# The part of the scan output that depends only on silu(z), computed among the scan inputs and added to x there

## Chip, core and metric

The kernel runs on one core of a Trainium2 chip. The metric is device time in microseconds of one execution; lower is better. Before the change it was 9031.49 us, the median of 3 runs (9028.09 to 9043.99).

## What is computed

Four layers run one after the other on 4 images of 64 x 64 tokens with 128 channels, all in f32: a Mamba-like block (layer 0), self-attention (layer 1), a convolution block (layer 2) and neighbourhood attention with an MLP (layer 3). The change lies in layer 0. Cut to what matters:

```python
xz = _ln(input) @ in_proj_w
x_, z = jnp.split(xz, 2, axis=-1)
xc = silu(depthwise_conv3x3(x_) + conv_b)
# four directions k: delta, B, C from xc; h = exp(delta*A)*h + delta*xc*B ; y_k = sum_n h*C
y = sum of the four directions, each put back in image order, plus Ds * xc
y = _ln(y, onorm_w, onorm_b)          # (y - mean) * rstd * onorm_w + onorm_b
y = y * silu(z)
x = input + y @ out_proj_w
x = x + gelu(_ln(x) @ fc1_w + fc1_b) @ fc2_w + fc2_b
```

The kernel splits `y @ out_proj_w` into two sums. With c the centred y, it is `rstd * ((c * onorm_w * silu(z)) @ out_proj_w) + (onorm_b * silu(z)) @ out_proj_w`. The second sum, called `pb` in the kernel, does not depend on the scan.

## The kernel before

**Program and order.** `network` (L1620) writes the whole program for one core, without loops on the chip. A scheduling layer then decides, from its own estimate of times and from priorities, in which order each engine's instructions stand; on the chip each engine works its queue in that order and waits on semaphores. A tile pool gives out buffers in turn; a tile that needs a buffer waits until all uses of the one before have ended.

**Stages.** `scan_inputs` (L277) makes, for one image, everything the scan needs, in 8 chunks of 512 tokens: layer norm (`layernorm_T`, L178), in_proj, the 3x3 convolution on TensorE with diagonal weights (L247), Silu (L359 for z into `sz`, L376 for `xc`), the projections to delta, B and C (`steps`, L296), and it stores `sz`, `xc`, `delta`, `du` and `bc` to DRAM. `selective_scan` (L438) runs the four directions in the order 0, 1, 3, 2, in units: one unit is a product dB on POOL (L485), two exponentials on ACT (L491), two scans on DVE (L493), and the product with C, on DVE (L498) or POOL (L506). TensorE sums over the state with the `pick` matmuls of L539. The last direction runs backwards, so the y of chunk 7 is the first to be finished. `scan_output` (L565) takes y, `sz` and x of each chunk from DRAM, chunk 7 first, two chunks interleaved, and makes the norm, the gate, out_proj, the second layer norm and the MLP (`mlp`, L212); meanwhile it also steps through `layer3_mlp` (L1552) of the image before. `rest` (L1588) is `scan_output`, `layer1`, `layer2` and layer 3's attention (`layer3_attention`, L1216) of one image.

**How they lie together.** The scans of the four images follow one another and have the high priority base `SCAN_FIRST` written around them. `scan_inputs` of image 0 comes first; those of images 1 to 3 are issued next to the scan of image 0, and `rest` of image i next to the scan of image i + 1. `rest` of image 3 and its MLP of layer 3 come after the last scan.

**Queues and buffers.** SP issues the loads of both stages and of the scan (`dt` and `du` L468, `bc` L476, `y_before` L520 to L530), the stores of `du` (L332), and the loads of x (L338 in `scan_inputs`, L594 in `scan_output`). ACT issues the stores of `sz`, `xc`, `bc` and `delta`. `bc`, `dt`, `du` and `dB` have 4 buffers each; the pool of `scan_inputs`, in which x lies, has 2. The scan holds 4 PSUM banks (3 `dA`, 1 `py`), the other stage 4, shared by all its tiles with the tag `ps`.

**The Silus.** `Together` (L100) gathers the activations of a chunk that need another table (Silu of z of chunk c, Silu of the convolution of chunk c - 1) and lets them run only after the last of their matmuls.

**The lines that the change touches.** In `scan_inputs` the weights are loaded at L288 to L291, x at L338, and `sz` is stored at L382. In `scan_output` the weights are loaded at L576 and L577, L580 scales `out_proj` by `onorm_b` on DVE, L594 loads x. L612 sums the squares (`pv`), L621 makes `pb`, L625 the gated part `pg`, L628 adds `pb` to x on DVE, and L630 adds `rstd * pg`.

Of the kernel before, what the change touches and what calls it, by code (L numbers as in the profile page):

```python
# [28 lines left out]
F32 = mybir.dt.float32  # L29
# [13 lines left out]
LC = 512  # L43
# [213 lines left out]
def token_tiles(dram, c):  # L257

    return dram[span(c), :].rearrange("(t p) c -> p t c", p=128)
# [17 lines left out]
def scan_inputs(tc, K, A, D, img):  # L277

    nc = tc.nc
    with ExitStack() as ctx:
        pool = ctx.enter_context(tc.tile_pool(name="si_a", bufs=2))
        wpool = ctx.enter_context(tc.tile_pool(name="si_aw", bufs=1))
        psum = ctx.enter_context(tc.tile_pool(name="si_ap", bufs=4, space=PSUM))
        load = loader(tc, wpool, A, 0)
        ln_w, ln_b = load("ln1_w", [128, 1]), load("ln1_b", [128, 1])  # L288
        in_proj, conv_b = load("in_proj_w", [128, 2 * DI]), load("conv_b", [128, ND])
        diag = load("conv_diag", [128, ND, 9, 128], D.conv_diag)  # L290
        x_proj, dt_w = load("x_proj_w", [128, ND, 2, 128]), load("dt_w", [128, 2, DI])  # L291
        xc = wpool.tile([128, ND, NT], F32, name="xc")
        together = Together(tc, K)
        bands = {}

        def steps(o, c):  # L296


            if o == 0:
                tk = xc[:, :, span(c)].rearrange("p d (a b) -> p d a b", b=H)  # L300
            else:
                tk = xc.rearrange("p d (h w) -> p d w h", w=W)[:, :, span(c, RC), :]
            px = psum.tile([128, LC], F32, name="ps")
            for d in range(ND):
                nc.tensor.matmul(
                    px.rearrange("p (a b) -> p a b", b=H), x_proj[:, d, o, :], tk[:, d, :, :],
                    start=(d == 0), stop=(d == ND - 1),
                )
            xdbl = pool.tile([128, LC], F32, name="xdbl")
            nc.scalar.activation(xdbl, px, AF.Identity, bias=K.first2)  # L310
            deltas = [pool.tile([128, ND, LC], F32, name="delta", bufs=2 if K.general else 3) for b in range(2)]
            for d in range(ND):
                pds = []
                for b in range(2):
                    pd = psum.tile([128, LC], F32, name="ps")
                    rows = slice(64 * b, 64 * b + 1 + R)
                    nc.tensor.matmul(
                        pd, dt_w[rows, o, d * 128 : (d + 1) * 128], xdbl[rows, :], start=True, stop=True
                    )
                    pds.append(pd)  # L320
                for b in range(2):
                    softplus(tc, K, pool, deltas[b][:, d, :], pds[b])
            for b in range(2):
                k, first = o + 2 * b, 64 * b + 1 + R
                nc.scalar.dma_start(D.bc[img][k][c].rearrange("n w t -> w n t"), xdbl[first : first + 2 * NS, :])
                nc.scalar.dma_start(D.delta[img][k][c], deltas[b])
                du = pool.tile([128, ND, LC], F32, name="du")
                nc.gpsimd.tensor_mul(  # L328
                    du.rearrange("p d (a b) -> p d a b", b=H),
                    deltas[b].rearrange("p d (a b) -> p d a b", b=H), tk,  # L330
                )
                nc.sync.dma_start(D.du[img][k][c], du)  # L332

        for c in range(NCH + 1):
            acts = []
            if c < NCH:
                xt = pool.tile([128, 4, 128], F32, name="x")
                nc.sync.dma_start(xt, token_tiles(A["x"][img], c))  # L338
                xnT = pool.tile([128, LC], F32, name="xnT")
                layernorm_T(tc, K, pool, psum, xt, ln_w, ln_b, xnT)  # L340
                band = pool.tile([128, ND, RC + 2, W], F32, name="band", bufs=3)
                bands[c] = band
                for d in range(ND):
                    ps = psum.tile([128, LC], F32, name="ps")
                    nc.tensor.matmul(ps, in_proj[:, d * 128 : (d + 1) * 128], xnT, start=True, stop=True)
                    rows = ps.rearrange("p (h w) -> p h w", w=W)
                    nc.scalar.copy(band[:, d, 1 : RC + 1, :], rows)
                    if c > 0:
                        nc.scalar.copy(bands[c - 1][:, d, RC + 1, :], rows[:, 0, :])
                        nc.scalar.copy(band[:, d, 0, :], bands[c - 1][:, d, RC, :])  # L350
                sz = pool.tile([128, ND, LC], F32, name="sz")
                for d in range(ND):
                    ps = psum.tile([128, LC], F32, name="ps")
                    mm = nc.tensor.matmul(
                        ps, in_proj[:, DI + d * 128 : DI + (d + 1) * 128], xnT, start=True, stop=True
                    )
                    if d == 0:
                        together.open(mm)
                    acts.append(lambda d=d, ps=ps, sz=sz: nc.scalar.activation(sz[:, d, :], ps, AF.Silu))  # L359
            if c > 0:  # L360

                b, src = c - 1, bands.pop(c - 1)
                top, bottom = (1 if b == 0 else 0), (RC + 1 if b == NCH - 1 else RC + 2)
                for d in range(ND):
                    ps = psum.tile([128, LC], F32, name="ps")
                    mm = conv3x3(
                        nc,
                        ps.rearrange("p (h w) -> p h w", w=W),
                        lambda t, d=d: diag[:, d, t, :],
                        src[:, d, top:bottom, :],  # L370
                        1 - top,
                        RC,
                        bottom - top,
                    )
                    acts.append(
                        lambda d=d, ps=ps, b=b: nc.scalar.activation(  # L376
                            xc[:, d, span(b)], ps, AF.Silu, bias=conv_b[:, d : d + 1]
                        )
                    )
            together.run(mm, acts)  # L380
            if c < NCH:
                nc.scalar.dma_start(D.sz[img][c], sz)  # L382
            if c > 0:
                nc.scalar.dma_start(D.xc[img][c - 1], xc[:, :, span(c - 1)])
                steps(0, c - 1)
        for c in range(NCH):
            steps(1, c)
# [177 lines left out]
def scan_output(tc, K, A, D, img, xT, last):  # L565
# [5 lines left out]
    with ExitStack() as ctx:  # L571
# [1 line left out]
        wpool = ctx.enter_context(tc.tile_pool(name="so_w", bufs=1))  # L573
        psum = ctx.enter_context(tc.tile_pool(name="so_p", bufs=4, space=PSUM))
        load = loader(tc, wpool, A, 0)
        onorm_w, onorm_b = load("onorm_w", [128, ND]), load("onorm_b", [128, ND])  # L576
        out_proj = load("out_proj_w", [128, ND, C])  # L577
        out_proj_b = wpool.tile([128, ND, C], F32, name="out_proj_b")
        for d in range(ND):
            nc.vector.tensor_scalar_mul(out_proj_b[:, d, :], out_proj[:, d, :], onorm_b[:, d : d + 1])  # L580
        center = wpool.tile([128, ND, 128], F32, name="center")
        nc.vector.memset(center, -1.0 / DI)
        nc.vector.tensor_add(center[:, 0, :], center[:, 0, :], K.ident)
# [4 lines left out]
        def chunk(c):  # L588
# [2 lines left out]
            sz = pool.tile([128, ND, LC], F32, name="sz")  # L591
            nc.sync.dma_start(sz, D.sz[img][c])
            x = pool.tile([128, 4, 128], F32, name="x")
            nc.sync.dma_start(x, token_tiles(A["x"][img], c))  # L594
            gated = pool.tile([128, ND, LC], F32, name="gated", bufs=1)
            ycs = []
            for d in range(ND):
# [16 lines left out]
                    )  # L614
            rstd = pool.tile([128, 4], F32, name="rstd")
            rstd_of(nc, K, rstd, pv)
            pb = psum.tile([128, 4, 128], F32, name="pb", tag="ps")
            pg = psum.tile([128, 4, 128], F32, name="pg", tag="ps")
            for t in range(4):
                for d in range(ND):  # L620
                    nc.tensor.matmul(  # L621
                        pb[:, t, :], sz[:, d, span(t, 128)], out_proj_b[:, d, :], start=(d == 0), stop=(d == ND - 1)
                    )
                for d in range(ND):
                    nc.tensor.matmul(  # L625
                        pg[:, t, :], gated[:, d, span(t, 128)], out_proj[:, d, :], start=(d == 0), stop=(d == ND - 1)
                    )
            nc.vector.tensor_add(x, x, pb)  # L628
            for t in range(4):
                nc.vector.scalar_tensor_tensor(  # L630
                    x[:, t, :], pg[:, t, :], rstd[:, t : t + 1], x[:, t, :], ALU.mult, ALU.add
# [988 lines left out]
def network(tc, A, out):  # L1620
    nc = tc.nc
    with ExitStack() as ctx:
# [10 lines left out]
        D.conv_diag = scratch("conv_diag", [128, ND, 9, 128])  # L1633
        D.w2_diag, D.w2_norms = scratch("w2_diag", [128, 20, 128]), scratch("w2_norms", [128, len(NORMS2), 4])
        D.w2_cv4, D.w2_bias = scratch("w2_cv4", [128, 128]), scratch("w2_bias", [1, 128])
        for name, shape in (("sz", [128, ND, LC]), ("xc", [128, ND, LC]), ("y", [128, ND, LC])):
            setattr(D, name, [[scratch(f"{name}{b}_{c}", shape) for c in range(NCH)] for b in range(B)])
        for name, shape in (("delta", [128, ND, LC]), ("du", [128, ND, LC]), ("bc", [NS, 2, LC])):
            made = [
# [113 lines left out]
```

## Time and profile before

| | us |
|---|---|
| median of 3 runs | 9031.49 |
| the profiled execution | 9043.9 |
| its span, first to last instruction | 9042.2 |
| PE busy (share of the span) | 7228.6 (80%) |
| DVE busy | 7119.0 (79%) |
| POOL busy | 7048.5 (78%) |
| ACT busy | 5646.5 (62%) |
| first dB of the scan (L485) starts | 120.5 |
| last in_proj matmul of `scan_inputs` (L354) starts | 1997.6 |
| first y load of `scan_output` (L590) starts | 2224.8 |
| last scan on DVE (L493) starts | 7895.5 |
| first matmul of image 3's layer 1 on the chain (L743) | 8199.2 |

All times come from one profiled execution of 9042.2 us. The rows that follow name the line, the engine, the operation, the tile written and the tiles read, the shapes and the count; behind the bar stand busy time in us, the mean of one in ns, and the idle time of the engine just before these instructions with what ended most of it. An f32 matmul appears as two records in the timeline and in the chain. The page's slices are fortieths of the span, 226 us each, with the busy share in tenths.

### The profile page before, as it was taken

To read this page: it belongs to the slowest core of one execution; us is meant where nothing else is said; L and a number is where in the kernel's file an instruction comes from. 1 tells how busy PE (TensorE), PEld (TensorE's weight loads), DVE (VectorE), ACT (ScalarE), POOL (GpSimd) and SP (SyncE) were. 2 spreads that over 40 slices of the span, in tenths; PEclk is the share of its full clock that TensorE was granted. 3 is DMA by queue.
4 is the path that set the end of the run, shared out by engine and by line. 5 is a ranking of instruction groups with operands and counts; after the bars stand their busy time and mean duration, and the time that the engine had idled before them with its cause. 6 is when DMAs were issued, how large, how long until landed. Compare 5 with 4: busy or idle time off the path is not lost. (4 is left out here: it accounts for less than half of the span.)

```text
span 9042.2 us, 99354 instructions
## 1 busy us (share of the span) xinstructions
PE 7228.6 (80%) x30116; PEld 2738.4 (30%) x30116; DVE 7119.0 (79%) x8483; ACT 5646.5 (62%) x11581; POOL 7048.5 (78%) x3064
## 2 busy tenths in 40 slices
PE   5835868686788997877788988877888978888987
PEld 2211213132422232333322333333222323343333
DVE  3888878787899988988899988888899898813433
ACT  5746767675666666657766665667666666554355
POOL 5988898999899979997899979988999799800000
PEclk8757868696898998888898988888999988889989
DMA  4777676777544445565444555565445465510020
GB/s 169 254 235 238 238 243 239 252 249 267 170 166 170 163 161 198 194 213 181 156 168 167 176 181 179 200 201 165 166 160 178 146 215 186 184 51 4 7 78 29
DMA packets 716655, 1581.74 MB, mean 175 GB/s; under 512 B 203317, under 2 KB 328396, under 8 KB 711757
## 3 DMA queue, kind: packets, MB, share of 16 engines
q1 hardware_dynamic: 585805, 1399.10, 45.3%
q10 hardware_dynamic: 130304, 176.19, 5.5%
q8 instruction: 241, 3.95, 0.2%
q14 instruction: 305, 2.50, 0.1%
HBM read 1280.47 MB, written 283.59 MB: 173 GB/s over the span
## 5 line engine op out<-in xcount | busy, mean ns | idle before, releaser
L485 POOL TENSOR_TENSOR dB<-du,bc 128x1024 f32<-128x1024 f32 x2048 | 4799.3, 2372 | 699.2 <-DMA bc<-bc_dram 263.0
L491 ACT ACTIVATE dA<-dt,w_A_log 128x512 f32<-128x512 f32 x4096 | 2782.4, 691 | 606.5 <-DVE hc L493 306.1
L493 DVE TENSOR_TENSOR_SCAN dA<-dA,state,dB 128x512 f32<-128x512 f32 x2128 | 2630.1, 1272 | 291.2 <-POOL dB L485 153.9
L493 DVE TENSOR_TENSOR_SCAN hc<-dA,state,dB 128x512 f32<-128x512 f32 x1456 | 1804.6, 1267 | 299.9 <-ACT dA L491 115.3
L506 POOL TENSOR_TENSOR hc<-hc,bc 128x1024 f32<-128x1024 f32 x832 | 1969.8, 2373 | 81.0 <-ACT state L502 55.8
L498 DVE TENSOR_TENSOR hc<-dA,bc 128x512 f32<-128x512 f32 x2432 | 1566.3, 675 | 129.7 <-PE py L539 114.0
L539 PE MATMUL py<-hc,pick 128*32 128x512 f32 x8192 | 1256.6, 693 | 388.0 <-POOL hc L506 273.3
L823 PE MATMUL pa<-e,l_v 128*128 128x512 f32 x2048 | 1083.6, 662 | 24.4 <-ACT e L779 24.3
L500 ACT COPY state<-dA 128x1 f32<-128x1 f32 x2128 | 328.7, 158 | 1207.9 <-DVE hc L498 1196.5
L775 PE MATMUL pair<-l_g,l_f 32*128 32x512 f32 x2048 | 539.2, 676 | 186.7 <-ACT e L779 136.3
L779 ACT ACTIVATE e<-pair 128x1024 f32<-128x1024 f32 (+1 forms) x448 | 508.4, 1135 | 236.5 <-PE pair L775 230.4
L823 PEld LDWEIGHTS pa<-e,l_v 128*128 128x128 f32 x2048 | 380.3, 202 | 691.8 <-issue 635.0
L539 PEld LDWEIGHTS py<-hc,pick 128*32 128x32 f32 x8192 | 213.4, 117 | 1152.9 <-issue 472.7
L1281 PE MATMUL pair<-table,ident 128*128 128x512 f32 x768 | 429.5, 687 | 114.3 <-ACT e L1291 95.5
L247 PE MATMUL ps<-band,w_conv_diag 128*128 128x504 f32 (+3 forms) x1152 | 500.8, 594 | 3.5 <-ACT delta L397 3.5
L493 DVE TENSOR_TENSOR_SCAN dA<-dA,dB 128x512 f32<-128x512 f32 x304 | 357.7, 1213 | 69.8 <-POOL dB L485 50.2
L201 PE MATMUL ps<-ident,ln_xn 128*128 128x128 f32 x512 | 134.6, 359 | 305.3 <-ACT ln_xn L198 198.1
L328 POOL TENSOR_TENSOR du<-delta,xc 128x1024 f32<-128x1024 f32 x128 | 334.7, 2622 | 49.3 <-ACT delta L397 47.8
L1291 ACT ACTIVATE e<-pair 128x1024 f32<-128x1024 f32 (+1 forms) x224 | 254.4, 1136 | 167.9 <-PE pair L1285 167.5
L219 PE MATMUL ps<-xnT,w_fc_w 128*128 128x512 f32 x512 | 277.5, 675 | 72.9 <-ACT mlp_h L226 33.4
L247 PEld LDWEIGHTS ps<-band,w_conv_diag 128*128 128x128 f32 x1152 | 221.6, 193 | 282.1 <-issue 263.1
L775 PEld LDWEIGHTS pair<-l_g,l_f 32*128 32x128 f32 x2048 | 140.6, 190 | 548.3 <-ACT e L779 262.2
(274 smaller groups left out, 8583.6 us busy)
## 6 DMA issues: line engine op xcount, KB each, us to landing
bc<-bc_dram SPq DMA_DIRECT2D x1024, 512.0 KB
dt<-delta_dram SPq DMA_DIRECT2D x512, 512.0 KB
du<-du_dram SPq DMA_DIRECT2D x512, 512.0 KB
delta_dram<-delta ACTq DMA_DIRECT2D x128, 512.0 KB
du_dram<-du SPq DMA_DIRECT2D x128, 512.0 KB
table<-biasT_dram SPq DMA_DIRECT2D x72, 512.0 KB
y_first_dram<-y_sum ACTq DMA_DIRECT2D x128, 256.0 KB
y_before<-y_first_dram SPq DMA_DIRECT2D x128, 256.0 KB
```

The costliest lines, as they stand in the source:

```text
L247: mm = nc.tensor.matmul(out[:, r0 - row0 : r1 - row0, c0:c1], lhsT((dy + 1) * 3 + dx + 1), src[:, r0 + dy : r1 + dy, c0 + dx : c1 + dx], s ...
L328: nc.gpsimd.tensor_mul(du.rearrange("p d (a b) -> p d a b", b=H), deltas[b].rearrange("p d (a b) -> p d a b", b=H), tk,)
L485: nc.gpsimd.tensor_mul(dB, dus[pp], mid(bct[:, 0, :], 2))
L491: nc.scalar.activation(dA, dts[pp][:, g, :], AF.Exp, scale=S.A[:, k, j, pr, g : g + 1])
L493: nc.vector.tensor_tensor_scan(hg[:, order], dA[:, order], dB[:, g, order], 0.0 if i == 0 else state[:, j, pr, g : g + 1], ALU.mult, ALU.add,)
L498: mm = nc.vector.tensor_mul(hc[:, g, :], dA, bct[:, 1, :])
L506: made.append(nc.gpsimd.tensor_mul(hc, hc, mid(bct[:, 1, :], 2)))
L539: mm = nc.tensor.matmul(py[0][32 * q : 32 * q + 32, :], S.pick, hcs[q // 2][:, q % 2, :], start=(k == 1 and j == 0), stop=(j == NJS - 1),)
L775: nc.tensor.matmul(ps[:, u, :], f[quad, t // 4, span(t % 4, 128)], g[quad, c, :], start=True, stop=True)
L779: made = nc.scalar.activation(e, ps, AF.Exp)
L823: nc.tensor.matmul(pa, v[:, 8 * q + t, :], es[q], start=(t == 0 and q == 0), stop=(t == 7 and q == 3),)
L1281: nc.tensor.matmul(ps[:, u, :], K.ident, t[:, u, :], start=True, stop=False)
```

## The change

The changed kernel makes `pb` in `scan_inputs`, as soon as `sz` of the chunk is there, adds it to the x tile that the layer norm has read, and stores the sum in a new DRAM scratch `xb`. `scan_output` loads `xb` in place of x and has neither `pb` nor its addition. The scaling of `out_proj` by `onorm_b` moves too, from DVE in `scan_output` to ACT in `scan_inputs`; `out_proj` is loaded in both stages.

```diff
@@ scan_inputs
         x_proj, dt_w = load("x_proj_w", [128, ND, 2, 128]), load("dt_w", [128, 2, DI])
+        onorm_b, out_proj_b = load("onorm_b", [128, ND]), load("out_proj_w", [128, ND, C])
+        for d in range(ND):
+            nc.scalar.activation(out_proj_b[:, d, :], out_proj_b[:, d, :], AF.Copy, scale=onorm_b[:, d : d + 1])
...
                 nc.scalar.dma_start(D.sz[img][c], sz)
+                pb = psum.tile([128, 4, 128], F32, name="pb", tag="ps")
+                for t in range(4):
+                    for d in range(ND):
+                        nc.tensor.matmul(
+                            pb[:, t, :], sz[:, d, span(t, 128)], out_proj_b[:, d, :],
+                            start=(d == 0), stop=(d == ND - 1),
+                        )
+                nc.vector.tensor_add(xt, xt, pb)
+                nc.sync.dma_start(D.xb[img][c].rearrange("(t p) c -> p t c", p=128), xt)
@@ scan_output
-        onorm_w, onorm_b = load("onorm_w", [128, ND]), load("onorm_b", [128, ND])
-        out_proj = load("out_proj_w", [128, ND, C])
-        out_proj_b = wpool.tile([128, ND, C], F32, name="out_proj_b")
-        for d in range(ND):
-            nc.vector.tensor_scalar_mul(out_proj_b[:, d, :], out_proj[:, d, :], onorm_b[:, d : d + 1])
+        onorm_w, out_proj = load("onorm_w", [128, ND]), load("out_proj_w", [128, ND, C])
...
-            nc.sync.dma_start(x, token_tiles(A["x"][img], c))
+            nc.sync.dma_start(x, D.xb[img][c].rearrange("(t p) c -> p t c", p=128))
...
-            pb = psum.tile([128, 4, 128], F32, name="pb", tag="ps")
             pg = psum.tile([128, 4, 128], F32, name="pg", tag="ps")
             for t in range(4):
                 for d in range(ND):
                     nc.tensor.matmul(
-                        pb[:, t, :], sz[:, d, span(t, 128)], out_proj_b[:, d, :], start=(d == 0), stop=(d == ND - 1)
-                    )
-                for d in range(ND):
-                    nc.tensor.matmul(
                         pg[:, t, :], gated[:, d, span(t, 128)], out_proj[:, d, :], start=(d == 0), stop=(d == ND - 1)
                     )
-            nc.vector.tensor_add(x, x, pb)
@@ network
-        for name, shape in (("sz", [128, ND, LC]), ("xc", [128, ND, LC]), ("y", [128, ND, LC])):
+        for name, shape in (("sz", [128, ND, LC]), ("xc", [128, ND, LC]), ("y", [128, ND, LC]), ("xb", [LC, C])):
```

## The prediction

> **What bounds the kernel now.** I read, in this order, the busy slices of the page, the sums by stage, the costliest rows, and then the chain of waits and PE's timeline at the end of the scan.
>
> ```profile
> PE   5835868686788997877788988877888978888987
> DVE  3888878787899988988899988888899898813433
> POOL 5988898999899979997899979988999799800000
> ```
>
> POOL is at 8 or 9 tenths until slice 35 and then does nothing: the span is a scan stage set by POOL and a tail set by something else. Sums by stage (the three stretches that I asked for; columns are length, then busy us and instructions of PE, PEld, DVE, ACT, POOL, then clock and DMA):
>
> ```profile
> 120.00:2240.00 2120.00, 1461.93 (x4648) 492.84 (x4649) 1733.34 (x1984) 1374.43 (x3105) 1898.02 (x811) 0.75 0.70 243
> 2240.00:7898.00 5658.00, 4746.91 (x20968) 1772.40 (x20967) 5019.97 (x5862) 3667.03 (x7514) 5114.67 (x2204) 0.88 0.52 178
> 7898.00:8198.00 300.00, 234.29 (x870) 133.36 (x871) 48.61 (x194) 160.84 (x337) 0.00 (x0) 0.88 0.17 53
> ```
>
> In both scan stretches POOL is the busiest, 90% of each; DVE is at 82 and 89%, PE at 69 and 84%. All four runs of `scan_inputs` lie in the first stretch, `rest` of images 0 to 2 in the second, `scan_output` of image 3 in the third, with PE at 78% and POOL out. So work moved out of the third stretch counts against the end, and work put into the first should lie beside POOL.
>
> ```profile
> L485 POOL TENSOR_TENSOR dB<-du,bc 128x1024 f32<-128x1024 f32 x2048 | 4799.3, 2372 | 699.2 <-DMA bc<-bc_dram 263.0
> L506 POOL TENSOR_TENSOR hc<-hc,bc 128x1024 f32<-128x1024 f32 x832 | 1969.8, 2373 | 81.0 <-ACT state L502 55.8
> ```
>
> 2048 units of the scan, each one dB, take POOL's time; its largest single wait is for `bc` loads (263 us in all), which SP issues. The chain of waits in the third stretch (start, us, what) shows who sets the tail:
>
> ```profile
> 7930.43 1.87 PE pv L612 x16
> 7932.29 2.09 PE pb L621 x12
> 7934.38 2.33 PE pg L625 x12
> ```
>
> `pb` is on the chain; its pieces between 7895 and 8200 add up to 18.3 us for 8 chunks, 2.3 us a chunk. DVE's addition of it is not on the chain: it only waits.
>
> ```profile
> L628 DVE TENSOR_TENSOR x<-x,pb 128x512 f32<-128x512 f32 x8 | 5.5, 687 | 63.6 <-PE pb L621 63.6
> ```
>
> Last, PE's timeline where image 2's `rest` ends (L1318 is its last matmul), the scan ends (L539) and image 3's output begins (L600):
>
> ```profile
> 7888.39 1.97 PE L1318 MATMUL pj<-w_proj_w,oT 128*128 128x128 f32 x8 [0.57 <-DVE oT L1314]
> 7890.30 2.72 PE L539 MATMUL py<-hc,pick 128*32 128x512 f32 x16
> 7898.20 1.94 PE L539 MATMUL py<-hc,pick 128*32 128x512 f32 x8 [5.18 <-DVE hc L498]
> 7904.63 5.85 PE L600 MATMUL ps<-y,center 128*128 128x512 f32 x8 [4.50 <-DMA y<-y_dram]
> ```
>
> `rest` of image 2 and the scan of image 3 end within 10 us of each other (an f32 matmul leaves two records, so 12 pick matmuls follow L1318), and the output stage starts after both.
>
> **What the Trainium skill says.** "TensorE: Matmul & The Clock Gate", Architectural detail: PE keeps its matmuls in order and only pulls weight loads ahead; so a `pb` that waits for sz holds up every matmul behind it. The trace agrees where L600 above waits 4.5 us for y. "DMA: Bandwidth & Descriptors", Anatomy of one DMA: about 2.0 us of a transfer is fixed, mostly the receipt of the write, and a wait for a semaphore stands on the issuing sequencer. Here a store of the same 256 KB (x_dram) took 2.16 us on the chain. "VectorE: DVE Perf Modes", Why PSUM operands drop a tier: a sum with a PSUM operand runs at the base rate; the trace has 674 ns for this 128x512 one, wherever it stands.
>
> **The change part by part.**
>
> Removed from the tail. Of image 3's 8 chunks each loses 8 matmuls of `pb`, 2.3 us of the chain: 18.3 us. Chunk 7's part falls in the overlap counted next, so 7 x 2.3 = 16 us. The eight additions (5.5 us) have PE as their late partner and give nothing on their own; the two scalings of L580 neither, as y is the later input.
>
> The earlier start. In the built programs' orders the last `pj` of image 2 stands before 12 pick matmuls of the scan now, and before 24 in the changed one, since its `scan_output` has lost its own `pb` (the first attention rows of image 2 already stand 12 earlier). Four pick matmuls belong to two units. A unit takes 5658 us / 1532 dB = 3.7 us, so `rest` of image 2 ends 6 x 3.7 = 22 us earlier against the scan. The orders also show chunk 7 of image 3 up to its first L219 ahead of the scan's last picks, where now it lies after them: L600 at 7904.6 is 4.5 us after the last pick, and the first L219 comes at 7924.35, 24 us after it. I take 20 us. What is late next is chunk 6's y, which is in DRAM by then.
>
> Added to the first stretch: per chunk 8 matmuls (2.3 us PE, 32 times 74 us), one addition (0.67, 22 us DVE), one 256 KB store (8.4 MB against 243 GB/s x 2120 us = 515 MB moved there), and per image two scalings on ACT (0.30 us each by L273's row, 5.35/18) and two loads, 0.43 us of SP each. POOL gets nothing, and PE has 31% free, DVE 18%. The second stretch loses 24 times the same: 55 us PE, 16 us DVE. Both balances lie beside POOL; I cost them at nothing. If that cover is gone, DVE's 6 us net is the price.
>
> Start-up, where nothing covers: before the first dB (120.5 us) the two scalings take 0.6 us ahead of the first Silu, and `pb` of chunks 0 and 1 stand on PE ahead of chunk 1's in_proj and of the first x_proj. Behind the second stands L305, which waits for the xc Silus anyway (1.3 us after sz's). At least 0, at most 0.6 + 2 x 2.3 = 5; I take 1.5 us.
>
> New waits. On DVE the addition waits for `pb`, scans queue behind it; it is placed some scans after the Silu, so the wait is short. `pb` also takes one of the four PSUM banks of the stage until DVE has read it, where only ACT freed them before; what is late by it is `scan_inputs` alone, which has the whole first stretch. On SP the store waits for the addition, and the load of x two chunks on, which now needs that store landed (the x pool has two buffers, and x is held to the end), often follows directly; behind both stand bc, dt and du, for which POOL and ACT wait. At least 2 us per chunk for 24 such pairs. bc has four buffers, each serving two units of 3.7 us, so a load has a unit or two to spare. Below nothing is possible too, since later x loads unblock other rows. Bounds -10 and +60; I take +3 us.
>
> The scan's own end: chunk 7's matmuls and DVE work now compete with its last units, 0 to 6; I take 2 us.
>
> Sum: -16 - 20 + 1.5 + 3 + 2 = -29.5 us. Against the profiled execution, 9043.9 us, that is 9014. It stands 12 us above the median of the runs, 9031.5, so the forecast is **9002 us**.
>
> **Rivals.**
>
> A, only the chain's part (0.17): the earlier start is given back, because PE and DVE were full at the scan's end and the output work pushed under it delays the last units. For it: PE was at 83% over the last 200 us. Against: the work before was as dense there. -16 + 6.5, so 9022 us.
>
> B, slower (0.13): SP's queue. If the store's wait and x's wait for its landing expose more than 1.6 us per chunk on POOL, 32 of them eat the 32.5 us of the other terms and 18 more. With 2.5 us each it is 80 us, less 32.5, so 9079 us. For it: bc already ends 263 us of POOL's idle time. Against: between 900 and 1800 us bc waits on POOL come to under 10 us, although four du stores per step already wait on SP in the same way.
>
> C, more (0.15): the scans of images 1 to 3 lose 16 us of DVE and speed up, as POOL waits for the scans' dB buffers there (`DVE hc L493` is its second releaser), and the start gains its full 24. -16 - 24 - 10 + 3, so 8985 us.
>
> **How the numbers follow.** The forecast has 0.55; its own range is 8985 to 9018. Down to 8972 takes in C, up to 9030 takes in A: that leaves B and little else out. About 0.2%, 18 us, can be told from no change, so faster means below 9013.4. Faster: 0.51 of the forecast, C's 0.15 and 0.04 of A, 0.70. Same: 0.04 of the forecast and 0.13 of A, 0.17. Slower: B, 0.13.
>
> **What would show it.** Right: in the stretch of about 300 us after the scan no `pb`, and some 35 us less from the last L539 to the first L743; L600 of image 3 before the last L539; the last L493 within 10 us of 7896; `pg` directly behind `pv` on the chain. Wrong: POOL's wait for bc before 2240 us grown by tens of us with SP waiting at the xb store or the x load (B); the last L493 well after 7905 while the tail is short (A or B); a first dB after 126 us (start-up mis-sized).

## The result, and the profile after

The changed kernel takes 9049.8 us (median of 19 runs, 9036.8 to 9068.3) against 9033.5 us for the kernel before on the same chip (19 runs). The ratio is 1.0016, 95% interval 1.0009 to 1.0022: about 15 us slower, where 29.5 us faster were forecast. The two profiled executions are nearly equally long (spans 9042.2 and 9041.6 us), because before's was a long one of its kind and after's a short one; so I use the traces for where things stand, and the runs for the sum. In the views PE is TensorE, DVE VectorE, ACT ScalarE, POOL GpSimd, and SP the engine that issues the loads and part of the stores.

The stretches that were shown of before, for the changed kernel (length, then busy us and instructions of PE, PEld, DVE, ACT, POOL, clock, DMA share, GB/s):

```profile
120.00:2240.00 2120.00, 1490.60 (x5096) 550.50 (x5097) 1741.20 (x2016) 1368.78 (x3104) 1877.61 (x803) 0.76 0.71 244
2240.00:7898.00 5658.00, 4694.92 (x20604) 1712.57 (x20596) 5001.25 (x5825) 3670.67 (x7523) 5114.06 (x2205) 0.88 0.52 179
7898.00:8198.00 300.00, 230.12 (x762) 127.91 (x762) 66.32 (x206) 166.85 (x347) 18.02 (x8) 0.85 0.18 56
```

In the first stretch PE has 29 us more and POOL, the busiest engine, has done 8 instructions fewer. In the last stretch POOL still has 18 us of work where it had none: the scan ends late. The last scan ends at 7929.4 us, before it was 7896.8. Two lines of the page, POOL's busy slices and the row of the product dB (busy, mean ns, idle before it):

```profile
POOL 5888898989799979997799979997899899900000
...
L497 POOL TENSOR_TENSOR dB<-du,bc 128x1024 f32<-128x1024 f32 x2048 | 4789.1, 2362 | 704.2 <-DMA bc<-bc_dram 217.5
```

POOL's idle time before its products is what it was (699.2 us), and less of it is ended by `bc` (263.0 before): the slower scan does not show in this sum over the span. PE's timeline where the scan ends (start, duration, idle before):

```profile
7895.18 1.93 PE L551 MATMUL py<-hc,pick 128*32 128x512 f32 x8 [2.91 <-POOL hc L518]
...
7908.26 3.67 PE L608 MATMUL ps<-y,center 128*128 128x512 f32 x8
7911.86 1.07 PE L551 MATMUL py<-hc,pick 128*32 128x512 f32 x8
...
7916.82 3.42 PE L620 MATMUL pv<-mean_col,y 128*128 128x1 f32 x16
7920.10 2.05 PE L628 MATMUL pg<-w_out_proj_w,gated 128*128 128x128 f32 x8
...
7928.41 1.92 PE L551 MATMUL py<-hc,pick 128*32 128x512 f32 x14
```

Image 3's output (L608, which was L600) now begins between the scan's last pick matmuls (L551) and not after them, as forecast, and no `pb` stands between `pv` and `pg`. But it begins at 7908 us, nearly as before (7905): it moved ahead against the scan, and the scan itself came 33 us later.

The chain of waits at the end of that stage:

```profile
8136.99 3.37 PE pv L620 x16
8140.36 0.02 issue
8140.39 0.27 ACT rstd L174
8140.66 0.02 issue
8140.68 0.21 ACT rstd L175
8140.90 3.17 issue
8144.06 1.12 DVE x L632 x4
```

Where the chain before ran `pv`, `pb`, `pg` on PE, it now leaves PE after `pv`, goes to ACT for `rstd` and on to the scaling on DVE. In this chunk the next thing that is late stood close behind `pb`.

To see when the scan fell behind I counted GpSimd's products in both traces (`dB`, the products with C, and the `du` of the inputs, all in order of time) and compared when each starts. The 80th starts at 322.7 us before and 341.0 after, 18.3 us late, in the middle of image 0's inputs. The delay then shrinks to 5 us at about 990 and swings between -1 and 25 us up to 2030. It is 27 us at about 2215, the end of the inputs before, 44 us at 2450, 60 us at 4230, and 33 us at the scan's end. So most of the delay of the start is made up, and most of what is missing at the end comes up later. SP's waits of the changed kernel in the first part, 20 to 345 us (us, times, longest), and then POOL's from 120 to 345, after and before:

```profile
SPq L394 <- DVE x L393: 63.6, 8, 18.6
...
SPq L341 <- DMA xb_dram<-x: 7.7, 4, 3.0
```

```profile
POOL dB L497 <- DMA du<-du_dram: 18.0, 1, 18.0
POOL dB L497 <- issue: 12.3, 2, 7.0
POOL dB L497 <- DVE dA L505: 12.0, 3, 5.8
POOL dB L497 <- DMA bc<-bc_dram: 11.2, 4, 5.2
```

```profile
POOL dB L485 <- DMA du<-du_dram: 25.7, 1, 25.7
POOL dB L485 <- DMA bc<-bc_dram: 16.8, 4, 8.7
...
POOL dB L485 <- DVE dA L493: 2.4, 2, 1.4
POOL dB L485 <- issue: 1.6, 1, 1.6
```

SP stands 64 of these 325 us at the store of `xb` (L394) until the addition (L393) is done, and loads of the first units queue behind it. Before, neither line existed. But this standing took the place of other waits: all waits of SP in this window add up to 253 us, and to 255 before. POOL's waits don't name the loads either. The one wait for `du` lies in front of the first product, and those for `bc` became shorter. Those for the scans on DVE (`dA` and `hc`) went from 9.5 to 12.0 us, and what grew most is "issue", for which the profile shows no reason. That the store makes the 80th product late is thus suggested by SP's queue, and not shown by POOL's waits.

### The profile page after: what moved, and what is told of

Same layout as the page of the kernel before. It is cut to its first block, busy times and chain, and to the rows that moved or that the text cites. A ratio compares the mean times of both kernels' runs of the same rounds, so it can differ in the third digit from the quotient of the medians.

```text
span 9041.6 us, 99365 instructions
## 1 busy us (share of the span) xinstructions
PE 7199.7 (80%) x30116; PEld 2732.9 (30%) x30116; DVE 7125.0 (79%) x8475; ACT 5651.1 (63%) x11589; POOL 7045.5 (78%) x3064
## 5 line engine op out<-in xcount | busy, mean ns | idle before, releaser
L551 PE MATMUL py<-hc,pick 128*32 128x512 f32 x8192 | 1248.7, 688 | 386.2 <-POOL hc L518 287.1
L551 PEld LDWEIGHTS py<-hc,pick 128*32 128x32 f32 x8192 | 214.5, 117 | 1152.5 <-issue 458.4
L233 PE MATMUL ps<-mlp_h,w_fc_w 128*128 128x512 f32 x512 | 274.1, 682 | 49.9 <-ACT mlp_h L226 49.9
```

The costliest lines, as they stand in the source:

```text
L551: mm = nc.tensor.matmul(py[0][32 * q : 32 * q + 32, :], S.pick, hcs[q // 2][:, q % 2, :], start=(k == 1 and j == 0), stop=(j == NJS - 1),)
```

## The experiments

Unless another kernel is named, ratios are to the kernel before on the same chip. "Scan's end" is the end of the last scan on DVE in the profiled execution, "late at the 80th" the delay of GpSimd's 80th product against before (322.7 us). The granted clock of the profiled executions lies between 0.854 and 0.864 in all runs and does not explain the differences (before 0.855, e1 0.858, e2 0.859, e7 0.858, e15 0.857). A single profiled execution can lie 10 to 20 us from the median of its runs: before's is 12 us above, e13's 21 above, e6's 14 below.

**e1, the saving alone.** `pb`, its addition and the scaling are left out of `scan_output`, and nothing is put in their place: that term of the sum is not computed.

```diff
-            pb = psum.tile([128, 4, 128], F32, name="pb", tag="ps")
-                for d in range(ND): nc.tensor.matmul(pb[:, t, :], sz..., out_proj_b...)
-            nc.vector.tensor_add(x, x, pb)
```

> The kernel before without pb, its addition and its scaling in scan_output, for all images, and nothing put in their place (the term with onorm_b is left out of the output). Theory 1 (the saving in the tail and at the start of the last output stage is real, and the work added to the scan inputs costs more): 25 to 45 us faster than before, the time from the last scan to the end shorter by about 33 us, as in the changed kernel. Rival (the saving itself is mostly given back elsewhere, for example by a scan that a denser rest slows): less than 15 us faster.

Measured 8973.5 us, ratio 0.9936 (0.9922 to 0.9950): 58 us faster, more than the 25 to 45 expected. The scan ends at 7873.6, 23 us earlier, and image 3's output begins at 7840, another 42 us earlier against the scan's end than before.

**e2, the cost alone.** The new work of `scan_inputs` is added to the kernel before; `scan_output` stays, nobody reads `xb`.

```diff
                 nc.scalar.dma_start(D.sz[img][c], sz)
+                pb = ...; 8 matmuls; nc.vector.tensor_add(xt, xt, pb); nc.sync.dma_start(D.xb[img][c]..., xt)
```

> The kernel before with pb, its addition and the store of xb put into scan_inputs, while scan_output stays as it was (the new tensor is not read). Theory 1: 35 to 60 us slower than before, all of it before the last scan ends. Rival (the two parts are not additive, it is the new order as a whole): within 20 us of before.

9107.1 us, ratio 1.0079 (1.0065 to 1.0093): 71 us slower, more than the 35 to 60 expected, the scan's end at 7955.2 (+58), 22.7 us late at the 80th. Saving and cost add up: -58 + 71 = +13 us against +15 for the whole change, with about 13 us of uncertainty on each of the two. So the 71 us are what has to be explained. The delay of GpSimd's products is 14 to 20 us at about 990, 40 at about 2200, where the inputs of the kernel before end, and 60 at 3000 and at the scan's end: most of it arises while the inputs run.

**e3, x free after the addition.** The sum is written into the tile `xnT`, which is done with by then; the next load of x no longer waits until the store has landed.

```diff
-                nc.vector.tensor_add(xt, xt, pb)
-                nc.sync.dma_start(D.xb[img][c]..., xt)
+                xb = xnT.rearrange("p (t c) -> p t c", c=128)
+                nc.vector.tensor_add(xb, xt, pb)
+                nc.sync.dma_start(D.xb[img][c]..., xb)
```

> The changed kernel, but the sum x + pb is written into the chunk's xnT tile and stored from there, so that the x buffer is free after the addition and the load of x two chunks on need not wait on SP for the store to land. Theory SP (the waits of the xb store and of the x load hold up bc, dt and du on SP): 15 to 40 us faster than the changed kernel. Rival (the work itself, or the second wait alone, costs): within 10 us of the changed kernel.

9029.6 us, ratio 0.9995 (0.9987 to 1.0004), so 19 us less than the changed kernel, as the SP theory expected. The x load's wait for the landing, 40.8 us of SP's time up to 2240 us in the changed kernel, is gone; that of the store for the addition is not:

```profile
SPq L395 <- DVE xnT L394: 58.7, 5, 20.6
```

(the same 20 to 345 us), and the 80th product is still 16.0 us late. At about 990 us GpSimd has made that up, and the scan ends 1 us after that of the kernel before: what is late at the 80th need not be late at the end. The order of the instructions on all five engines changed with this edit too, so that the 19 us are the landing's is likely, not shown.

**e4, image 3 only.** The change is made for the last image, whose saving lies in the tail.

```diff
+        early = img == B - 1
```

> The change for image 3 alone; images 0 to 2 have pb in scan_output as before. Theory 1: the tail gains its 16 us of pb, rest of image 2 does not end earlier, and only 8 of 32 chunks add work to the inputs: 5 to 20 us faster than before. Rival (what costs is the order around image 0 and the start of rest, hardly the amount): no gain, or slower than before.

9044.6 us, ratio 1.0011 (1.0005 to 1.0018): 10 us slower where 5 to 20 faster were expected. GpSimd is not late at the 80th (-2.1) and 15 us late at about 2000, during image 3's inputs, but the scan ends 2 us earlier than before. The trace, 12 us under the median of its runs, does not show where the 10 us lie.

**e5 and e10, the store and the addition written later.** In e5 the store of chunk c stands behind the load of chunk c + 1 in the program; in e10 the addition stands behind `steps` as well.

```diff
+            if c > 0: nc.sync.dma_start(D.xb[img][c - 1]..., xb)      # e5
                 steps(0, c - 1)
+            if c < NCH: nc.vector.tensor_add(xb, xt, pb)             # e10
```

> The changed kernel with the sum in the xnT tile (as in e3), and the store of chunk c's sum issued one chunk later, just after chunk c+1's x load, so that the SP queue never stands at a store whose addition is not done. SP theory (the remaining loss is SP standing about 130 us at the store for the addition, with bc, dt and du loads and du stores behind it): a further 20 to 40 us faster than e3 (9029.6), so 8990 to 9010. Rival, TensorE and VectorE order (the eight extra matmuls and the addition stand in front of the work that feeds GpSimd): within 8 us of e3. Both: the scan's end moves forward by what the total gains.

> e5 with the addition alone issued behind the chunk's projections; its matmuls stay in front. VectorE theory: the matmuls are long done when VectorE reaches the addition, so its wait (38 us in e5) falls under 15 us and the last scan ends 20 to 45 us before e5's 7909, as in e8 (7861); time 5 to 30 us under e5. TensorE order theory (e8 gained because the matmuls moved): like e5 within 8 us, last scan end at 7900 to 7915.

9030.8 us (ratio 0.9999, 0.9991 to 1.0007) and 9029.3 us (0.9993, 0.9985 to 1.0002), both as e3. They say nothing on either theory: in the built programs every engine's instructions stand in exactly the order of e3, since the scheduling layer puts these two instructions where it wants them, wherever the text has them. What the two runs do give is a measure of repeats. Three times the same program: medians within 1.5 us, spans of the profiled executions from 9024.2 to 9034.4, the scan's end from 7898 to 7909. A difference of 10 us between two single traces is therefore none.

**e6, e7, e13, taking e2 apart.** e6 has only the matmuls, with no reader; e7 the matmuls and the addition into `xnT`, no store; e13 has in its place a copy of 4 columns of `pb`. None uses the result.

```diff
                 8 matmuls into pb
+                nc.vector.tensor_add(xnT..., xt, pb)                  # e7
+                nc.vector.tensor_copy(xnT[:, 0:4], pb[:, 3, 124:128]) # e13
```

> The kernel before with only the 256 extra matmuls in the inputs (and the scaling of the weights); nothing reads them, no addition, no store. TensorE theory: at 2.3 us a chunk in TensorE's order, most of the 73 us of e2 is already there, 40 to 75 us slower than before. SP theory: 0 to 15 us slower, since the store and the addition are absent.

> The kernel before with the extra matmuls and the addition (into the xnT tile, which nobody reads afterwards) in the inputs, without the store. VectorE theory (the addition's wait for the matmuls holds the scans queued behind it): 20 us or more over e6. SP theory: within 8 us of e6, and 30 to 60 us under e2 (9107).

> e7 with VectorE reading 4 columns of pb (128x4, into the xnT tile) in place of the whole addition; matmuls as in e6 and e7, no store, nothing uses the result. PSUM bank theory (pb keeps one of the stage's four banks until its reader comes by in VectorE's order): 50 to 90 us slower than before, near e7 (9123). VectorE time theory (32 x 0.67 us and the scans behind them): 0 to 25 us slower than before, near e6 (9039).

e6: 9039.1 us, ratio 1.0006 (0.9999 to 1.0012). e13: 9074.0, 1.0042 (1.0029 to 1.0055). e7: 9123.1, 1.0102 (1.0087 to 1.0116). e6 falls in the range of the SP theory, e7 in that of the VectorE theory, e13 between its two. The program with the matmuls alone, 74 us of PE, is about 5 us slower, which can't be told from nothing, although its image 0 output begins at 2294 us, as late as in the changed kernel (2290; before 2230): a later start of that output alone does not cost. With a reader of 0.16 us each the program is 38 us slower, with the whole addition 92. The store is not needed for a cost of this size: without it e7 is even slower than e2. POOL's waits for the scans' buffers between 120 and 2240 us do not settle it: 72.5 us in e6 and 119.5 in e7, but 124.8 before, with neither.

The tiny read of e13, with what its engine waited for and who waited for it:

```profile
L393 DVE COPY xnT<-pb x32: 135/162/164, 63.4 to 2042.0; 128x4 f32<-128x4 f32 x32
...
its engine sat idle before it (us, times) until:
  PE pb L389: 57.5, 18
who waited for it (us, times):
  POOL dB L496: 13.7, 6
```

DVE idles 57.5 us in front of 5 us of work, and GpSimd waits for it six times. But most of the 57.5 us lie before the scan starts (19.5 and 18.7 us ahead of the first two reads), and only part of the cost is seen in the inputs: in e13 GpSimd is 18 us early at 2450 us and the scan ends at 7901.8, yet image 3's output begins 48 us after that. In e7 it begins 68 us after the scan's end, before it was 8. The code of `rest` is that of the kernel before in both. So the order was dealt differently there too: the scheduling layer sorted the whole program anew, and other instructions than the added ones moved. In e7's trace, against that of before, 24 us lie at the scan's end and 60 in the later start behind it; in e13's 5 and 40; in e2's 58 and 6. The split into 5, 38 and 92 us is that of whole programs, not of the instructions alone.

**e14, the addition alone.** Both operands in SBUF, no matmuls, no store, result unused.

```diff
+                xb = xnT.rearrange("p (t c) -> p t c", c=128)
+                nc.vector.tensor_add(xb, xt, xb)
```

> The kernel before with the addition alone in the inputs, both operands in SBUF (x and the xnT tile, whose content is overwritten after its last use), no matmuls, no store, result unused. VectorE time theory: 40 to 90 us slower than before. PSUM bank or matmul theory: within 15 us of before.

9075.2 us, ratio 1.0049 (1.0036 to 1.0062): 44 us. It looks like proof of the VectorE theory and is none, because this is another instruction than the one with `pb`:

```profile
L387 DVE TENSOR_TENSOR xnT<-x,xnT x32: 666/1342/5521, 55.5 to 2024.2; 128x512 f32<-128x512 f32 x32
```

(minimum, median, maximum in ns). In the changed kernel the addition takes 660 to 689 ns. The timeline shows why:

```profile
1484.88 2.36 POOL L490 TENSOR_TENSOR dB<-du,bc 128x1024 f32<-128x1024 f32 x1
1485.58 2.21 DVE L387 TENSOR_TENSOR xnT<-x,xnT 128x512 f32<-128x512 f32 x1 [2.38 <-PE ps L357]
```

The addition starts while a product of GpSimd runs, and ends 0.55 us after that. "SBUF — State Buffer", Who interferes with whom, has it: a VectorE instruction with two SBUF inputs and a GpSimd instruction that reads SBUF exclude one another, and the second waits for the first. The trace agrees: the additions that met no product took 0.67 to 0.69 us, and the longest, 5.52 us, outlasted two whole products. Three additions began 0.07 to 0.23 us before a product; they took 0.67 to 0.68 us, and the product 2.65 to 2.82 in place of 2.36. The 32 took 50.6 us in place of 21.8. So in e14 51 us more on DVE, with some longer products, went with 44 us, and it stays open what 22 us cost.

**e8, matmuls and addition behind the projections.** On top of e5; this time the order does change.

```diff
+                steps(0, c - 1)
+            if c < NCH: pb = ...; 8 matmuls; nc.vector.tensor_add(xb, xt, pb)
```

> e5 with the extra matmuls and the addition issued behind the chunk's own projections and softplus (steps) and not in front of them. TensorE order theory: the projections no longer wait 2.3 us a chunk, 15 to 40 us faster than e5. Rival (TensorE's time counts wherever it stands in the inputs, or the SP queue is all of it): within 8 us of e5.

9021.6 us, ratio 0.9988 (0.9979 to 0.9996), 9 us under e5, less than the 15 to 40 expected and hardly clear of the two intervals. The addition hardly waits for its matmuls: 1.4 us in all after 120 us, against 21.6 in e5 and 16.7 in the changed kernel. SP's wait at the store in 20 to 345 us:

```profile
SPq L343 <- DVE xnT L401: 22.7, 7, 13.6
```

The 80th product is 4.2 us late in place of 16 to 18.5, and the scan ends at 7861, 36 us before that of the kernel before. Image 3's output now begins 32 us after the scan's end, so most of this is not collected.

**e9 and e11, the sum on TensorE and ACT.** TensorE adds x by four more matmuls with the identity, ACT copies the sum; e9 on e5, e11 on e8.

```diff
+                    nc.tensor.matmul(pb[:, t, :], K.ident, xt[:, t, :], start=True, stop=False)
-                nc.vector.tensor_add(xb, xt, pb)
+                nc.scalar.copy(xb, pb)
```

> e5 with the addition taken off VectorE: TensorE adds x into pb by four more matmuls with the identity, and ACT copies the sum into the xnT tile. VectorE theory (VectorE standing at the addition for its matmuls, 38 us in e5, delays the scans and so GpSimd): the last scan ends 20 to 50 us before e5's 7909, and the time is 10 to 40 us under e5 (9030.8). TensorE or inputs-length theory (the inputs stage ends later, at about 2290 to 2310 us, and image 0's output with it): within 8 us of e5, or slower by the added matmuls.

> e8 (matmuls and sum behind the projections) with the sum made by TensorE and ACT as in e9. If VectorE's own 22 us and its wait are what is left: 5 to 25 us under e8 (9021.6). If the later start of image 0's output (2300 us in e8, 2230 before) is what is left: within 8 us of e8, with that start still at 2290 to 2310.

9119.6 us (1.0096, 1.0080 to 1.0112) and 9067.3 us (1.0039, 1.0025 to 1.0053): 89 and 46 us over the kernels that they were made from, which neither expectation of the two had allowed. They also have 128 more matmuls and an order dealt anew, so they do not price ACT alone; but taking the addition off VectorE did not save its cost. At the 80th GpSimd is 12 and 25 us late although SP waits under 6 us for the sum in both. A late start thus has more than one cause.

**e12, a control.** Only the two loads and two scalings in each image's inputs, unread.

```diff
+        onorm_b, out_proj_b = load(...), load(...)
+        for d in range(ND): nc.scalar.activation(out_proj_b[:, d, :], ..., scale=onorm_b[:, d : d + 1])
```

> The kernel before with only the two extra weight loads and the two scalings on ACT in the inputs of each image; nothing reads them. It sizes what a small edit does by dealing the instructions anew. If the differences of the earlier runs are due to their work: within 6 us of before, last scan end within 8 us of 7897, image 0's output within 8 us of 2230. If any edit re-deals the order by tens of us: 15 us or more away in time or in one of the two places.

9027.5 us, ratio 0.9994 (0.9987 to 1.0002), no difference in time. Yet in its trace image 3's output begins 24 us before the scan's end, before 8 us after it. An edit with next to no work moves the order that far, and here it cost nothing.

**e15, e17, e16, e18, which images.** e15 is the change for images 1 to 3, e17 for image 0 alone; e16 is e8's form for images 0 to 2, e18 for images 1 to 3.

```diff
+        early = img > 0        # e15, e18; e17: img == 0; e16: img < B - 1
```

> The changed kernel for images 1 to 3 only; image 0 as before. Start theory (image 0's inputs pace the scan's first units: GpSimd was 18 us late at 323 us in the changed kernel): that delay is gone, within 4 us of before at 323 us, and the time is 10 to 20 us under the changed kernel (9050) although image 0's saving in its output (a quarter of 58 us) is lost: 9030 to 9040. Rival (delays of the start are made up later, since the order leaves room): 9045 to 9065.

> The changed kernel for image 0 only; images 1 to 3 as before: the complement of e15. Start theory with parts that add up: +16 = x - 48, so 50 to 75 us slower than before, GpSimd 10 to 20 us late at 323 us and the last scan's end 20 us or more after 7897. Rival (e15 is fast by its own deal of the order, image 0's part costs what it did at 323 us less its saving): -5 to +20 us.

> e8 (sum into the xnT tile, stored one chunk later, matmuls and addition behind the projections) for images 0 to 2 only; image 3 as before. If image 3's part costs more than it saves, as e4 (11 us slower) suggests: 5 to 20 us under e8, 9002 to 9017. If image 3's part of e8 pays by the shorter tail: 5 to 15 us over e8.

> e8's form (sum into the xnT tile, stored one chunk later, matmuls and addition behind the projections) for images 1 to 3; image 0 as before. If the form and the choice of images add up: 10 to 30 us under e15 (8984.7), 8955 to 8975. If e8's form only mended image 0's start, which is as before here: within 8 us of e15.

| | us | ratio (95%) | late at the 80th | scan's end | image 3's output begins |
|---|---|---|---|---|---|
| changed kernel | 9049.8 | 1.0016 (1.0009, 1.0022) | 18.3 | 7929 | 7908 |
| e15, images 1 to 3 | 8984.7 | 0.9951 (0.9938, 0.9965) | -0.4 | 7897 | 7827 |
| e17, image 0 | 9047.9 | 1.0018 (1.0011, 1.0026) | 18.9 | 7922 | 7902 |
| e16, e8 for 0 to 2 | 9008.7 | 0.9971 (0.9960, 0.9983) | 1.2 | 7857 | 7885 |
| e18, e8 for 1 to 3 | 8987.3 | 0.9957 (0.9943, 0.9971) | 0.8 | 7897 | 7854 |

e15 is 44 us faster than before and 59 us under the changed kernel (0.0065 of 9033 us), the best of all that compute the whole; e18 equals it within its interval. Leaving image 0 alone takes the delay at the 80th away, as the start theory said, and the scan ends where it did before. But the time is 45 us below that theory's range, and e17 alone is only 16 us slower, where parts that add up would need about 59. Nor is e17's delay at the 80th handed on: it is 0 to 9 us at about 990, GpSimd is 17 us early at 1800, and the 25 us at the scan's end come up after that. e16 and e18 fell in one of their two ranges each, e18 in that without a gain over e15. The 43 us that do not add up go with the order. PE's timeline of e15 shows it:

```profile
7816.18 1.94 PE L554 MATMUL py<-hc,pick 128*32 128x512 f32 x8 [2.31 <-POOL hc L521]
7827.32 6.35 PE L617 MATMUL ps<-y,center 128*128 128x512 f32 x8 [9.20 <-DMA y<-y_dram]
7833.60 1.92 PE L554 MATMUL py<-hc,pick 128*32 128x512 f32 x16
```

Image 3's output (L617) begins when GpSimd has started 2034 of the scan's 2048 `dB`, 69 us before the scan's end; in the changed kernel when it has started 2046, 21 us before it. From that start to the end of the program it is between 1120 and 1149 us in all these traces, while the start itself lies between 7827 and 7998, so the start sets most of the time.

## Why the prediction was wrong

**The step that failed** is "Both balances lie beside POOL; I cost them at nothing", with the start and SP terms beside it. For all that the inputs gain, the sum had 1.5 (start) + 3 (waits) + 2 (the scan's end) = 6.5 us; e2 measured 71. For all that the outputs lose it had -36; e1 measured -58. The sum was thus 64.5 us short on one side and 22 on the other, and the difference of these, 42.5 us, is nearly the whole error of about 45. That the cost lies in what the inputs gain is shown by e1 and e2. By which path the 71 us arise, a wait, a queue or the order dealt anew, stays open.

**POOL's load was not the limit of what an insertion costs.** In the first stretch before, POOL was busy 1898 us of 2120 (five of its first 35 slices read 5 or 7 tenths, not 8 or 9) and idle the rest, of which its products waited 125 us for scans on DVE. An instruction put into DVE's order ahead of scans may lengthen those waits, although DVE has 18% free. Rival C counted with just this wait, for the DVE time that the later scans save; the sum left it out for the DVE time that the inputs gain. The matmuls alone do fit (e6), so "PE has 31% free" held. The jump comes with a reader that joins PE's order to DVE's (e13, e7), but in these two most of it lies behind the scan's end, where the order put image 3's output. In e2 most lies in the scan, yet up to 2240 us POOL's waits for the scans are 128 us, and for `bc` 32, against 125 and 37 before; what grew is "issue", from 5 to 25 us, whose reason the profile does not show. So this path is possible and not shown, and in e9, with ACT as the reader, the cost was no smaller.

**Rival B's wait is there, its price is not shown.** The price taken was 3 us and the range allowed -10 to +60. Three programs with SP's wait at the store of about 60 us in the first 345 us (the changed kernel, e2, e3) have GpSimd 16 to 23 us late at the 80th product, and e17 with 57 us has 19; e8 and e16 with 23 us have 4 and 1; e6, e13 and e7 without the store have -1, 4 and 9. Against it stand e9 and e11, 12 and 25 us late with under 6 us of this wait, and that in the changed kernel, e3 and e17 the delay is mostly made up later (not in e2). B's mark, POOL's wait for bc grown by tens of us, did not come: it fell from 36.5 to 29.7 us up to 2240. For the x load behind the landed store e3 has 19 us, with another order.

**The first dB came as forecast,** 1.8 us late against 1.5. But I took it for the whole start, while image 0's inputs go on feeding the scan for another 200 us and more, and there the 18 us arose, most of which were made up later.

**The earlier start of image 3's output held:** 20 us against the scan's end were forecast, 29 came (from 8 after it to 21 before it). From the last pick matmul to the first matmul of layer 1 it is 271 us in place of 300, 29 less where some 35 were forecast. Both were eaten up by a scan that ended 33 us late where 2 were forecast. The mark "the last L493 well after 7905 while the tail is short", named for A or B, is what was found.

**`pb` on the tail's chain** was put at 16 us. From image 3's first center matmul to the first of its layer 1, the traces in which that output starts after the scan's end take 295 to 299 us with `pb` (before, e2, e6, e7, e13, e14, e16) and 285 to 293 without it (e3, e4, e5, e8, e9, e10): about 8 us. In the changed kernel it is 297, as the scan's last units lie inside. The mark "`pg` directly behind `pv` on the chain" did not come: the chain shows `rstd` next in line.

**Rival C was right about the effect:** the scans do speed up when `rest` has less to do, by 23 us at the scan's end in e1 where 10 were allowed. That it is DVE's 16 us which do it was not taken apart: e1 also frees PE and has another order.

**Left open:** how the 71 us divide between the reader's wait, its time, SP's queue and the order dealt anew, and why the order puts image 3's output 14 `dB` before the scan's last in e15 and 68 us after its end in e7. A run that keeps the old order by hand and inserts only the new instructions would tell it; it wasn't tried.

## What to carry to other kernels

Measure a move in two halves, what is removed alone and what is added alone: here they were -58 and +71 us, added up to the result, and showed at once which half was mispriced. (By images the parts did not add up, so adding up is to be tested, not taken for granted.) A free share of an engine's time is no price for work put into it: it was right here for matmuls without a reader (5 us for 74), and wrong for the whole of matmuls, reader and store. A delay at one point of a trace should be followed to the end before it is called a cost. Where a scheduling layer sets the order, look first whether an edit moved an instruction at all, and try the change on a part of its uses: leaving out image 0 turned 15 us lost into 44 us gained.

## What the runs showed of the hardware that was not expected

An addition of two SBUF tiles on VectorE beside GpSimd's products took 0.67 to 5.52 us, median 1.34, where the same addition with one operand in PSUM took 0.66 to 0.69 each time. 23 of the 32 took longer than 0.7 us. Moving an operand from PSUM to SBUF can thus make an instruction slower.
